# A GRU after attention on one core: input parts two steps at a time, accumulated in the gates' own PSUM banks

## The chip, the cores and the metric

The kernel runs on one core of a Trainium2 chip. The metric is the device time of one execution in microseconds (us). All arithmetic is in f32.

## The reference

Two layers with residual connections work on x of shape (16, 256, 512): batch B = 16, T = 256 steps, D = 512.

```python
x = x + _L0_cond_ref(x, cond[:, None, :], ...)   # normalisation, attention with 16 heads, o + o @ W_out
x = x + _L1_cond_ref(cond, x, W_ih, W_hh, b_ih, b_hh)

def cell(h, x):                                  # one step of the second layer, a GRU over T
    gi = x @ W_ih + b_ih                         # the input part
    gh = h @ W_hh + b_hh                         # the state part
    i_r, i_z, i_n = jnp.split(gi, 3, axis=-1)
    h_r, h_z, h_n = jnp.split(gh, 3, axis=-1)
    r = jax.nn.sigmoid(i_r + h_r)
    z = jax.nn.sigmoid(i_z + h_z)
    n = jnp.tanh(i_n + r * h_n)
    return (1.0 - z) * n + z * h
```

The first state is cond. The n gate's input part must stay apart from its state part, since only the state part is multiplied by r. Of r and z only the sum of both parts is needed. The 256 steps depend on each other through h.

## The kernel before, in words

The kernel has two stages. The attention stage takes the 16 batches one after the other; it ends at about 620 us in the profiled execution. The recurrent stage then runs the 256 steps. PE, DVE, ACT and POOL each follow the order in which the program was written (`manual_schedule`), so an instruction that waits holds all those behind it on its engine. SP issues the DMAs.

In the recurrent stage everything is held turned: the 512 features lie on 128 partitions in KC = 4 chunks, and 16 steps by 16 batches in the free dimension (`xT`, one tile for TI = 16 steps). Blocks of TG = 8 steps of x come in by DMA (`load_block`, six tiles `xin`), and DVE turns them into `xT` (`put_block`, L728). `output_step` (L713) makes the attention's output product for the next 16 steps in PSUM, and `put_output` (L746, DVE) adds it to `xT`. `input_step` (L713) makes the input parts `gi` for the next 16 steps: the weights `wih` are stationary, 128 x 32, and `xT` moves, 256 columns (16 steps x 16 batches); ACT adds the bias on the way out of PSUM (L757).

A step runs in this order.

1. PE: the state parts of r, n, z (`state_part`, L775). h is stationary, 128 x 16 for each k; the weights `whh` move, 128 columns, into four 32-column strips of the array, so 16 matmuls a gate. Each gate has one PSUM bank, of which 16 of every 32 rows are used.
2. DVE turns each gate back in 32 x 32 blocks (`turned`, L787), adds `gi` for r (L848), multiplies the state part of n by r (L851) and adds `gi` (L854), turns z and adds `gi` (L857).
3. ACT: sigmoid of r (L849), tanh of n (L855), sigmoid of z (L858). It also puts the n gate's hidden bias into its PSUM bank for the next step (`put_bhn`, L770).
4. PE, meanwhile: FILL = 4 steps of the products for the next 16 steps, by `output_step` or `input_step`.
5. DVE: three operations make the new h (L876 to L878). POOL adds h to x for the output (L880). Every eight steps DVE turns a block of output (L795) and SP stores it.

The group of the first 16 steps has no earlier steps to be made beside, so its `gi` is made before the first step; the last 16 steps have no next group to make.

An f32 matmul of the program is two instructions in the profile, and the four strips' matmuls go side by side.

Of the kernel before, what the change touches and what calls it, by code (L numbers as in the profile page):

```python
# [14 lines left out]
P = 128  # L15
# [4 lines left out]
def kernel(  # L20
# [35 lines left out]

    oT = const.tile([P, KC, T, B], F32, name="oT")
    wo = const.tile([P, KC, D], F32, name="wo")
    xin = ctx.enter_context(tc.tile_pool(name="xin", bufs=6))


    ada_a = const.tile([P, KC, B], F32, name="ada_a")
# [2 lines left out]
    gk_col = const.tile([P, 1], F32, name="gk_col")  # L65


    cond_sb = const.tile([KC * B, P], F32, name="cond_sb")
    for k in range(KC):
        nc.scalar.dma_start(cond_sb[k * B : (k + 1) * B, :], cond[:, k * P : (k + 1) * P])  # L70
    h0T = const.tile([P, KC, B], F32, name="h0T")

    work = ctx.enter_context(ExitStack())
    p1 = work.enter_context(tc.tile_pool(name="p1", bufs=1))
# [50 lines left out]
    def tile_ps(name, bank, shape=(P, D)):  # L125
        pool = ps if len(bank) == 1 else ps_lg
        return pool.tile(list(shape), F32, tag=bank, name=name)
# [313 lines left out]
    def slot2(b, w, prev, st):  # L441
        m = b + 1
        k = project(m, 1, 1, range(KC), "Y")
        maxima(w, range(HG))
        st.qk0 = norm_qk(m, 0, (st.q, st.k), st.rstd)
        st.v0 = project(m, 0, 2, (0,), "A")
        exps(w, range(HG))
        st.s1.add(0, st.sq)
        sq = st.s1.square(1, k)
        turn(prev)  # L450
        put_turned(prev, "vava")
        project(m, 0, 2, (1,), st.v0)
        st.s1.add(1, sq)
        if b + 3 < B:
            norm_first(b + 3, (1,))
        st.s1.rs.first()
        if b + 3 < B:
            batches[b + 3].rs.first()
        weigh(prev, "X")
        put_weighed(prev)  # L460
        if b == 0:

            for c in range(KC):
                d = wo[:, c, c * P : (c + 1) * P]
                nc.vector.tensor_tensor(d, d, ident, ALU.add)
        st.accs = (st.q1, k)
        st.rstd = st.s1.rs.second()
        normalize(w)
# [88 lines left out]
    with tc.manual_schedule(engines=ORDERED):  # L557
# [13 lines left out]
        for k in range(KC):  # L571
            for j in range(4):
# [4 lines left out]
                    start=(k == 0),  # L577
                    stop=(k == KC - 1),
                )
        cols = const.tile([P, 38], F32, name="cols")  # L580
        tp = tile_ps("tp_rows", "Y")
        nc.tensor.transpose(tp[:, :12], rows, ident[:12, :12])
        norm_first(0)
# [89 lines left out]
                    r = 32 * j + B * s  # L673
                    nc.sync.dma_start(xins[i][r : r + B], in_blocks(x, i, j, s))

    for i in range(6):
        load_block(i)


# [7 lines left out]
    gru = ctx.enter_context(tc.tile_pool(name="gru", bufs=2))  # L687


    bhn_rows = gru.tile([P, P], F32, name="bhn_rows", bufs=1)  # L690
    wide = gru.tile([P, KC, 32], F32, name="bhn_wide", bufs=1)
    nc.vector.tensor_copy(wide, bcols[:, 20:24].unsqueeze(2).to_broadcast([P, KC, 32]))
    nc.vector.transpose(bhn_rows, wide.rearrange("p q b -> p (q b)"))

    gates = []
    for name, bank in (("r", "A"), ("z", "X"), ("n", "Y")):
        gt = tile_ps(f"g{name}", bank, (P, P))
        nc.vector.memset(gt, 0.0)  # L700
        gates.append(gt)

    NI = T // TI
    NM = 3 * KC
    FILL = (KC + NM) * KC // TI
    gis = {}
    xTs = {}
    acc = {}

    def product(acc, w, m, k, rhs):  # L710

        for j in range(4):
            nc.tensor.matmul(  # L713
                acc[32 * j : 32 * j + 32, :],
                w[:, k, m * P + 32 * j : m * P + 32 * j + 32],
                rhs,
                start=(k == 0),
                stop=(k == KC - 1),
            )

    def put_block(i):

        grp, half = divmod(i, TI // TG)
        if half == 0:
            xTs[grp] = gru.tile([P, KC, TI, B], F32, tag="xT", name=f"xT_{grp}", bufs=3)
        nc.vector.transpose(  # L728
            xTs[grp][:, :, half * TG : (half + 1) * TG, :].rearrange("p q (s i) b -> p i q s b", s=2),
            xins[i],  # L730
        )
        load_block(i + 6)

    def output_step(grp, i):

# [9 lines left out]
        a = xTs[grp][:, m].rearrange("p t b -> p (t b)")  # L745
        nc.vector.tensor_tensor(a, o or acc["o"], a, ALU.add)  # L746

    def input_step(grp, i):

        m, k = divmod(i, KC)  # L750
        if i == 0:
            gis[grp] = gru.tile([P, NM, TI, B], F32, tag="gi", name=f"gi_{grp}")
        if k == 0:
            acc["i"] = tile_ps(f"gi_{grp}_{m}", ("Z", "lg2")[m % 2], (P, TI * B))
        product(acc["i"], wih, m, k, xTs[grp][:, k].rearrange("p t b -> p (t b)"))
        if k == KC - 1:
            nc.scalar.activation(  # L757
                gis[grp][:, m].rearrange("p t b -> p (t b)"), acc["i"], AF.Identity,
                bias=bcols[:, m : m + 1],
            )  # L760

    def open_hn():

        for j in range(4):
            nc.tensor.matmul(
                gates[2][32 * j : 32 * j + 32, :], ident[:, 0:32], ident, start=True, stop=True
            )

    def put_bhn():
        nc.scalar.copy(gates[2], bhn_rows)  # L770

    def state_part(g, hT):
        for k in range(KC):
            for j in range(4):
                nc.tensor.matmul(  # L775
                    gates[g][32 * j : 32 * j + B, :],
                    hT[:, k, :],
                    whh[:, k, g * D : (g + 1) * D].rearrange("p (q j c) -> p j q c", q=KC, c=32)[:, j],
                    start=(k == 0 and g != 2),
                    stop=(k == KC - 1),  # L780
                    skip_group_check=(g == 2),
                )

    def turned(g, t):

        tr = gru.tile([P, KC, 32], F32, tag=f"tr{g}", name=f"tr{g}_{t}")
        nc.vector.transpose(tr.rearrange("p q b -> p (q b)"), gates[g])  # L787
        return tr[:, :, 0:B]

    done = None  # L790

# [28 lines left out]
            queue.dma_start(dst[0, :, q], ol[0:B, q])  # L820

    with tc.manual_schedule(engines=ORDERED):
        for i in range(TI // TG):
            put_block(i)
        for i, o in enumerate(first):
            a = xTs[0][:, 2 * i : 2 * i + 2].rearrange("p q t b -> p q (t b)")
            nc.vector.tensor_tensor(a, o, a, ALU.add)  # L827
        for i in range(TI // TG, 2 * TI // TG):
            put_block(i)
        for i in range(NM * KC):  # L830
            input_step(0, i)
        open_hn()
        put_bhn()
        hT = h0T
        for t in range(T):
            tl = t % TG
            grp, ti = divmod(t, TI)
            gi = gis[grp]
            if tl == 0:
                y = gru.tile([P, KC, P], F32, tag="y", name=f"y_{t}", bufs=3)  # L840
            for g in (0, 2, 1):
                state_part(g, hT)

            def tile_of(name):
                return gru.tile([P, KC, B], F32, tag=name, name=f"{name}_{t}")

            r = tile_of("r")
            nc.vector.tensor_tensor(r, turned(0, t), gi[:, 0:KC, ti, :], ALU.add)  # L848
            nc.scalar.activation(r, r, AF.Sigmoid)  # L849
            n = tile_of("n")  # L850
            nc.vector.tensor_tensor(n, turned(2, t), r, ALU.mult)  # L851
            if t + 1 < T:
                put_bhn()
            nc.vector.tensor_tensor(n, n, gi[:, 2 * KC : 3 * KC, ti, :], ALU.add)  # L854
            nc.scalar.activation(n, n, AF.Tanh)  # L855
            z = tile_of("z")
            nc.vector.tensor_tensor(z, turned(1, t), gi[:, KC : 2 * KC, ti, :], ALU.add)  # L857
            nc.scalar.activation(z, z, AF.Sigmoid)  # L858


            ready = []
            if grp + 1 < NI:
                for i in range(FILL * ti, FILL * (ti + 1)):
                    if i < KC * KC:
                        output_step(grp + 1, i)
                        if i % KC == KC - 1:
                            ready.append((i // KC, acc["o"]))
                    else:
                        input_step(grp + 1, i - KC * KC)

            if t == T - 1:
                store_last(y, 0, TG - 1)


            h = gru.tile([P, KC, B], F32, tag="h", name=f"h_{t}", bufs=4)
            nc.vector.tensor_tensor(h, hT, n, ALU.subtract)  # L876
            nc.vector.tensor_tensor(h, h, z, ALU.mult)
            nc.vector.tensor_tensor(h, h, n, ALU.add)  # L878
            hT = h
            (nc.gpsimd if t + 1 < T else nc.vector).tensor_tensor(  # L880
                y[:, :, tl * B : (tl + 1) * B], xTs[grp][:, :, ti, :], h, ALU.add
            )
            for m, o in ready:
                put_output(grp + 1, m, o)
            block = t // TG + 2 * TI // TG
            if tl == TG - 2 and block < T // TG:
                put_block(block)
            if tl == 4 and done is not None:
                store(*done)
                done = None  # L890
            if tl == TG - 1:
                done = (t // TG, y)
        store_last(y, TG - 1, 1)
# [32 lines left out]
```

## Time and profile before

| | |
|---|---|
| time, median of 3 runs | 1775.45 us (1774.55 to 1776.77) |
| time of the profiled execution | 1775.52 us |
| span of its profile | 1773.7 us |
| PE busy | 1729.7 us, 98% |
| DVE busy | 1126.3 us, 64% |
| ACT busy | 816.9 us, 46% |
| POOL busy | 316.8 us, 18% |
| mean granted TensorE clock | 0.996 |
| first state part of step 0 | 644.22 us |
| first state part of step 1 | 648.57 us |
| first state part of the last step | 1763.54 us |

Span times count from the first instruction to the last; the profiled execution's own time is 1.8 us longer. A busy engine is not always the one that sets the end: PE's matmul ends are modelled, and whether PE or the loop through h sets a step must be read from the order of a step's instructions in time. Lines such as L775 are those of the kernel before; in the changed kernel the same functions stand at other lines.

### The profile page before, as it was taken

How to read it: one execution, taken by the hardware profiler on the slowest of the kernel's cores; microseconds unless marked ns; L12 is line 12 of the kernel's file. 1: busy time of each engine (PE TensorE's matmuls, PEld its weight loads, DVE VectorE, ACT ScalarE, POOL GpSimd, SP SyncE). 2: the span in 40 equal slices, each digit the busy share in tenths (PEclk: the TensorE clock that was granted, in tenths of full speed). 3: DMA queues.
4: the chain of work that ended last, by engine and by line, in shares of the span. 5: the costliest groups of instructions: out<-in, count | busy, mean ns of one | idle time of the engine just before them, and what ended most of it. 6: DMA issues, size and time to landing. Idle time of an engine off the chain costs nothing.

```text
span 1773.7 us, 91931 instructions
## 1 busy us (share of the span) xinstructions
PE 1729.7 (98%) x40755; PEld 1189.8 (67%) x40755; DVE 1126.3 (64%) x3703; ACT 816.9 (46%) x2760; POOL 316.8 (18%) x771
## 2 busy tenths in 40 slices
PE   7999999999999999999999999999999999999975
PEld 2444444444444578888888888888888888888865
DVE  4777777777776635656656656666556566665555
ACT  4777777777777623233233332333332332333322
POOL 0333344433344400000000000000000000000000
PEclk9999999999999899999999999999999999999999
DMA  8100000000000110100110011011101100000000
GB/s 286 38 14 14 14 26 14 14 14 23 5 3 2 73 27 16 22 16 16 22 22 16 17 23 20 16 20 22 17 16 21 22 10 10 16 10 10 10 15 14
DMA packets 146221, 43.72 MB, mean 25 GB/s; under 512 B 137899, under 2 KB 138031, under 8 KB 145823
## 3 DMA queue, kind: packets, MB, share of 16 engines
q1 hardware_dynamic: 145351, 36.73, 8.9%
q8 instruction: 320, 5.24, 1.2%
q10 hardware_dynamic: 472, 1.10, 0.2%
q14 instruction: 78, 0.64, 0.1%
HBM read 29.41 MB, written 8.39 MB: 21 GB/s over the span
## 4 chain that ended last, share of the span: by engine, by line
PE 94%; DVE 3%; ACT 1%; issue 1%; DMA 1%; DVEq 0%; ACTq 0%
PE qkv L214 19%; PE gi L713 18%; PE gr L775 13%; PE gn L775 13%; PE gz L775 11%; PE o L713 6%; PE tpa L188 4%; PE lg L279 4%; PE o L358 4%; PE tpqk L188 1%; DVE tr L787 1%; ACT attn L301 1%; PE tpx L188 1%; PE first L506 0%; DMA x<-in_x_dram 0%
## 5 line engine op out<-in xcount | busy, mean ns | idle before, releaser
L713 PE MATMUL gi<-xT,wih 128*32 128x256 f32 x6144 | 364.7, 379 | 0.0
L214 PE MATMUL qkv<-wq,xnT 128*32 128x512 f32 x3072 | 356.3, 598 | 0.6 <-DVE xnT L206 0.6
L312 POOL TENSOR_SCALAR attn<-attn,rden 128x256 f32<-128x256 f32 x510 | 234.1, 484 | 378.5 <-DVE rden L309 254.6
L775 PE MATMUL gr<-whh,h 128*16 128x128 f32 x8160 | 272.2, 274 | 24.1 <-DVE h L878 23.6
L880 POOL TENSOR_TENSOR y<-xT,h 128x64 f32<-128x64 f32 x255 | 82.0, 321 | 1068.0 <-DVE h L878 1033.1
L775 PEld LDWEIGHTS gr<-whh,h 128*16 128x16 f32 x8160 | 200.5, 96 | 107.1 <-DVE h L878 107.1
L775 PE MATMUL gz<-whh,h 128*16 128x128 f32 x8160 | 269.5, 273 | 0.0
L775 PE MATMUL gn<-whh,h 128*16 128x128 f32 x8160 | 269.5, 273 | 0.0
L301 ACT ACTIVATE attn<-lg,neg 128x256 f32<-128x256 f32 x512 | 234.9, 484 | 66.1 <-DVE neg L295 49.1
L713 PEld LDWEIGHTS gi<-xT,wih 128*32 128x32 f32 x6144 | 195.7, 110 | 101.3 <-DVE xT L827 0.7
L849 ACT ACTIVATE r<-r 128x64 f32<-128x64 f32 x256 | 65.7, 257 | 378.7 <-DVE r L848 378.7
L787 DVE STREAM_TRANSPOSE tr<-gr 128x128 f32<-128x128 f32 x256 | 81.1, 317 | 237.7 <-PE gr L775 237.7
L775 PEld LDWEIGHTS gn<-whh,h 128*16 128x16 f32 x8160 | 224.7, 97 | 0.0
L775 PEld LDWEIGHTS gz<-whh,h 128*16 128x16 f32 x8160 | 224.7, 97 | 0.0
L214 PEld LDWEIGHTS qkv<-wq,xnT 128*32 128x32 f32 x3072 | 87.4, 109 | 182.4 <-issue 157.3
L295 DVE TENSOR_REDUCE neg<-lg 128x2 f32<-128x512 f32 x256 | 159.1, 683 | 49.8 <-PE lg L279 49.8
L757 ACT ACTIVATE gi<-gi,cols 128x256 f32<-128x256 f32 x192 | 91.2, 475 | 164.1 <-PE gi L713 157.6
L787 DVE STREAM_TRANSPOSE tr<-gn 128x128 f32<-128x128 f32 x256 | 81.2, 317 | 76.0 <-PE gn L775 76.0
L341 DVE COPY attnT<-tpa 128x512 f32<-128x512 f32 x128 | 82.4, 682 | 59.2 <-ACT sq L225 34.6
L713 PE MATMUL o<-oT,wo 128*32 128x256 f32 x1920 | 114.6, 379 | 0.0
L855 ACT ACTIVATE n<-n 128x64 f32<-128x64 f32 x256 | 65.5, 256 | 98.5 <-DVE n L854 97.2
L301 ACT ACTIVATION_READ_ACCUMULATOR attn<-lg,neg 128x1 f32 x512 | 110.6, 216 | 0.0
(106 smaller groups left out, 1728.4 us busy)
## 6 DMA issues: line engine op xcount, KB each, us to landing
x<-in_x_dram SPq DMA_DIRECT2D x16, 512.0 KB, 4.0
xin<-in_x_dram SPq DMA_DIRECT2D x256, 32.0 KB, 2.0
out_dram<-osb SPq DMA_DIRECT2D x248, 32.0 KB, 1.8
wq<-in_L_cond_W_qkv_dram SPq DMA_DIRECT2D x12, 256.0 KB, 4.7
wih<-in_L_cond_W_ih_dram SPq DMA_DIRECT2D x4, 768.0 KB
whh<-in_L_cond_W_hh_dram SPq DMA_DIRECT2D x4, 768.0 KB
we<-in_L_cond_W_emb_dram SPq DMA_DIRECT2D x2, 512.0 KB, 4.8
we<-in_L_cond_W_emb_dram ACTq DMA_DIRECT2D x2, 512.0 KB
```

Of the source, the lines that this page charges most:

```text
L188: nc.tensor.transpose(dst[r], src[q], ident[q, q])
L214: nc.tensor.matmul(a[32 * j : 32 * j + 32, :], batches[b].xnT[:, k, n * P + 32 * j : n * P + 32 * j + 32], wq[:, k, s * D : (s + 1) * D], ...
L279: nc.tensor.matmul(w.lg[i][:, n, :], qT[r, g, n * P : (n + 1) * P], kT[r, g, :], start=True, stop=True,)
L295: nc.vector.tensor_reduce(w.neg[:, i, :], w.lg[i], AX.X, ALU.max, negate=True)
L301: nc.scalar.activation(a[:, n, :], w.lg[i][:, n, :], AF.Exp, bias=w.neg[:, i, n : n + 1], accum_out=w.den[:, i, n : n + 1],)
L312: engine.tensor_scalar(w.attn[i][:, n, :], w.attn[i][:, n, :], w.rden[:, i, n : n + 1], 1.0, ALU.mult, ALU.mult,)
L341: (nc.scalar.copy if engine is nc.scalar else nc.vector.tensor_copy)(dst, w.turned[i])
L713: nc.tensor.matmul(acc[32 * j : 32 * j + 32, :], w[:, k, m * P + 32 * j : m * P + 32 * j + 32], rhs, start=(k == 0), stop=(k == KC - 1),)
L757: nc.scalar.activation(gis[grp][:, m].rearrange("p t b -> p (t b)"), acc["i"], AF.Identity, bias=bcols[:, m : m + 1],)
L775: nc.tensor.matmul(gates[g][32 * j : 32 * j + B, :], hT[:, k, :], whh[:, k, g * D : (g + 1) * D].rearrange("p (q j c) -> p j q c", q=KC, c ...
L787: nc.vector.transpose(tr.rearrange("p q b -> p (q b)"), gates[g])
L880: (nc.gpsimd if t + 1 < T else nc.vector).tensor_tensor(y[:, :, tl * B : (tl + 1) * B], xTs[grp][:, :, ti, :], h, ALU.add)
```

## The change

The input parts are no longer made for 16 steps ahead and kept in SBUF. They are made for pairs of steps, one pair ahead, with x as the stationary operand (128 x 32: two steps of 16 batches) and the weights `wih` moving, 128 columns. They are accumulated in the PSUM banks in which the state parts follow. For r and z, input and state part sum up in the bank. The n gate's bank has two halves: the input part (with its bias) and the state part (with its bias).

- Each gate has two banks, for even and odd pairs. ACT seeds the banks of the next pair with the biases (`seed`, three copies every second step). `open_gate` does this by matmul for the first two pairs.
- In the first step of a pair the state part goes to rows 0 to 15 of each 32; in the second to rows 16 to 31, for which h is written into the second half of a tile whose first half is zero (`padded`), so that its stationary operand is 32 columns wide.
- DVE no longer adds `gi` to r and z; ACT reads the turned gate. In the first step of each pair DVE also turns the n gate's input half (`ni`), ahead of the turn of r, for both steps.
- Per step PE fills with one output step, two steps earlier than a step's share would be, and six input parts. Before the loop only the first pair's parts are made, and the rest of the first blocks' work moves into steps 0 and 1.
- `xin` has four tiles instead of six. The bias rows are made in the attention stage (`slot2` of batches 1 to 4, two small DVE operations each). The sigmoid table is loaded on ACT at the start of the stage.

```diff
+    gates = [
+        [tile_ps(f"g{name}_{i}", banks[i], (P, w, P)) for i in range(2)]
+        for name, banks, w in (("r", ("A", "lg2"), 1), ("z", ("X", "lg3"), 1), ("n", "ZY", 2))
+    ]
...
+    def seed(p):
+
+        nc.scalar.copy(gates[R_][p % 2][:, 0, :], b_rows[:, 0, :])
+        nc.scalar.copy(gates[N_][p % 2], b_rows[:, 2:4, :])
+        nc.scalar.copy(gates[Z_][p % 2][:, 0, :], b_rows[:, 1, :])
+
+    def gate_part(dst, rows, w, g, k, stationary):
         for j in range(4):
             nc.tensor.matmul(
+                dst[32 * j : 32 * j + rows, :],
+                stationary,
+                w[:, k, g * D : (g + 1) * D].rearrange("p (q j c) -> p j q c", q=KC, c=32)[:, j],
+                start=False,
+                stop=True,
+                skip_group_check=True,
             )
...
+    def input_part(p, g, k):
+
+        grp, ti = divmod(2 * p, TI)
+        x2 = xTs[grp][:, k, ti : ti + 2, :].rearrange("p t b -> p (t b)")
+        gate_part(gates[g][p % 2][:, 0, :], 32, wih, g, k, x2)
+
+    def state_part(t, g, hT):
+
+        dst = gates[g][t // 2 % 2]
         for k in range(KC):
+            gate_part(dst[:, dst.shape[1] - 1, :], hT.shape[2], whh, g, k, hT[:, k, :])
...
+            if s == 0 and p > 0 and more:
+                seed(p + 1)
+            if t > 0:
+                for g in (R_, N_, Z_):
+                    state_part(t, g, padded[p % 2] if s else hT)
...
+            gr, gz, gn = (gates[g][p % 2] for g in range(3))
+            if s == 0:
+                ni = turned("i", t, gn[:, 0, :])
             r = tile_of("r")
-            nc.vector.tensor_tensor(r, turned(0, t), gi[:, 0:KC, ti, :], ALU.add)
-            nc.scalar.activation(r, r, AF.Sigmoid)
+            nc.scalar.activation(r, turned("r", t, gr[:, 0, :])[:, :, s, :], AF.Sigmoid)
             n = tile_of("n")
-            nc.vector.tensor_tensor(n, turned(2, t), r, ALU.mult)
-            if t + 1 < T:
-                put_bhn()
-            nc.vector.tensor_tensor(n, n, gi[:, 2 * KC : 3 * KC, ti, :], ALU.add)
+            nc.vector.tensor_tensor(n, turned("h", t, gn[:, 1, :])[:, :, s, :], r, ALU.mult)
+            nc.vector.tensor_tensor(n, n, ni[:, :, s, :], ALU.add)
             nc.scalar.activation(n, n, AF.Tanh)
             z = tile_of("z")
-            nc.vector.tensor_tensor(z, turned(1, t), gi[:, KC : 2 * KC, ti, :], ALU.add)
-            nc.scalar.activation(z, z, AF.Sigmoid)
+            nc.scalar.activation(z, turned("z", t, gz[:, 0, :])[:, :, s, :], AF.Sigmoid)
...
+            for u in range(t + 2 if t else 0, t + 3):
+                if u // TI + 1 < NI:
+                    output_step(u // TI + 1, u % TI)
+                    if u % KC == KC - 1:
+                        ready.append((u // TI + 1, u % TI // KC, acc["o"]))
+            if more:
+                for g, k in parts[6 * s : 6 * s + 6]:
+                    input_part(p + 1, g, k)
...
-            h = gru.tile([P, KC, B], F32, tag="h", name=f"h_{t}", bufs=4)
+            if s == 0:
+                h = padded[p % 2][:, :, B:]
+            else:
+                h = gru.tile([P, KC, B], F32, tag="h", name=f"h_{t}", bufs=4)
```

## The prediction

> **What bounds the kernel now.** I read the page first, then one step of the recurrent stage in the timeline, then the two ends of that stage. The change touches nothing else of weight, so only these decide.
>
> The page's chain and its groups say PE, but not how narrowly:
>
> ```profile
> PE 94%; DVE 3%; ACT 1%; issue 1%; DMA 1%; DVEq 0%; ACTq 0%
> L775 PE MATMUL gr<-whh,h 128*16 128x128 f32 x8160 | 272.2, 274 | 24.1 <-DVE h L878 23.6
> ```
>
> The second line is the one to distrust: PE idles only 24.1 us for h over 255 steps, which looks like a PE bound. One step in the timeline (start, duration, engine, line) shows that it is not:
>
> ```profile
> 920.79 1.07 PE L775 MATMUL gr<-whh,h 128*16 128x128 f32 x32
> ...
> 921.92 0.32 DVE L787 STREAM_TRANSPOSE tr<-gr 128x128 f32<-128x128 f32 x1 [0.57 <-PE gr L775]
> 922.27 0.22 DVE L848 TENSOR_TENSOR r<-tr,gi 128x64 f32<-128x64 f32 x1
> ...
> 922.59 0.26 ACT L849 ACTIVATE r<-r 128x64 f32<-128x64 f32 x1 [1.10 <-DVE r L848]
> 922.80 0.32 DVE L787 STREAM_TRANSPOSE tr<-gn 128x128 f32<-128x128 f32 x1 [0.30 <-PE gn L775]
> ...
> 923.22 0.23 DVE L851 TENSOR_TENSOR n<-tr,r 128x64 f32<-128x64 f32 x1
> ...
> 923.48 0.22 DVE L854 TENSOR_TENSOR n<-n,gi 128x64 f32<-128x64 f32 x1
> 923.67 0.32 DVE L787 STREAM_TRANSPOSE tr<-gz 128x128 f32<-128x128 f32 x1
> 923.80 0.26 ACT L855 ACTIVATE n<-n 128x64 f32<-128x64 f32 x1 [0.38 <-DVE n L854]
> 924.02 0.23 DVE L857 TENSOR_TENSOR z<-tr,gi 128x64 f32<-128x64 f32 x1
> 924.16 0.22 DVE L876 TENSOR_TENSOR h<-h,n 128x64 f32<-128x64 f32 x1
> 924.34 0.26 ACT L858 ACTIVATE z<-z 128x64 f32<-128x64 f32 x1 [0.29 <-DVE z L857]
> 924.63 0.23 DVE L877 TENSOR_TENSOR h<-h,z 128x64 f32<-128x64 f32 x1 [0.25 <-ACT z L858]
> 924.89 0.22 DVE L878 TENSOR_TENSOR h<-h,n 128x64 f32<-128x64 f32 x1
> 925.17 0.68 PEld L775 LDWEIGHTS gr<-whh,h 128*16 128x16 f32 x28 [0.32 <-DVE h L878]
> ```
>
> A step is 925.17 - 920.79 = 4.38 us, and the next gr begins 0.06 after the last add of h: the chain ends last. The ends of the stage prove it, the first fence being its start, the second a step near its end:
>
> ```profile
> 623.26 20.93 PE L713 MATMUL gi<-xT,wih 128*32 128x256 f32 x384
> 644.00 0.40 PE L765 MATMUL gn<-ident 128*32 128x128 f32 x8
> 644.22 1.06 PE L775 MATMUL gr<-whh,h0T 128*16 128x128 f32 x32
> 646.84 1.91 PE L713 MATMUL o<-oT,wo 128*32 128x256 f32 x32
> 648.57 1.06 PE L775 MATMUL gr<-whh,h 128*16 128x128 f32 x32
> ```
>
> ```profile
> 1746.02 1.07 PE L775 MATMUL gr<-whh,h 128*16 128x128 f32 x32 [1.56 <-DVE h L878]
> ```
>
> In the last 16 steps PE has no filling work and waits 1.56 us each, yet they too last 4.38. So the chain is 4.38 and PE's own work fits in it almost exactly. PE's paces: each f32 matmul is two instructions, and four (one for each 32-column strip) go as a set. At 256 columns 96 sets take 644.00 - 623.26, or 0.216 us each. At 128 columns the 24 state sets take 646.84 - 644.22, or 0.109. A step's PE work is 24 x 0.1092 + 8 x 0.2158 = 4.35.
>
> **PE's work after.** The input parts turn from 256 columns (x moving) to 128 (weights moving), twice as many: per step 24 state sets, 12 input sets and 2 output sets, 36 x 0.1092 + 2 x 0.2158 = 4.36 us. Halving the columns costs 2 x 0.1092 - 0.2158 = 0.003 per pair of sets, about 0.01 a step. The Trainium skill speaks against it: "TensorEngine Tiling (Array Packing)", Instruction Overhead, puts about 60 cycles on each matmul; an estimate at the 2.4 GHz of "TensorE: Matmul & The Clock Gate" is 25 ns for each of six added sets a step, 0.15 us. The paces above leave no room for that, so I use them.
>
> The stationary operand becomes 32 columns wide for the input parts and for the state parts of odd steps (padded h); it is 16 now. The nearest row is L765, 32 wide at 128 columns: two sets from 644.00 to 644.22, the same 0.11. Its loads last 110 ns against 97 for 16 columns, which is just the pace of a set, so I take nothing and keep 3 ns a set as the upper bound. A gain is excluded, since columns already set the pace.
>
> **The chain in odd steps** (second of a pair). The additions at L848 and L857 go. Offsets from the start of gr: tr r 1.13 to 1.45 and straight to ACT, off the path, because the n gate is turned only at 2.01. Then n x r 2.43, n add 2.69, tanh 3.01 to 3.26, tr z 2.88 to 3.20. Sigmoid z starts at 3.29 instead of 3.55 (a DVE result reaches ACT in 0.10). Multiply 3.58, add 3.84 to 4.07, next gr 4.12. PE needs 4.36, so PE ends last: 4.36.
>
> **The chain in even steps** holds the cost. There a third transpose, ni, stands first on DVE. In the built order it waits for the last matmul of the n gate's *state* part, though it reads only the input half: both halves are one tile in one bank. The two transposes behind it carry no wait of their own, which fits only if the first one's wait covers the state part. So the turn of r, ready at 1.13, stands in the queue until 2.01, and ACT's sigmoid r waits for it. The "PSUM — Partial Sum Buffer" page, section Terms, gives a reason to keep such accesses apart: two engines on one bank and quadrant at once are an error there; no run here shows that.
>
> Working it out: DVE starts independent work about 0.08 before the former ends (z add 924.02, h subtract 924.16), so a transpose follows another after 0.24. ni 2.01, tr r 2.25 to 2.56, sigmoid r 2.66 to 2.91, tr n done 2.80. n x r starts 2.95 (ACT to DVE is 0.03), against 2.43 now. n add 3.21; tr z 3.35 to 3.67; tanh 3.53 to 3.78; sigmoid z 3.80 to 4.05 behind it. The subtract comes at 3.81 to 3.88 (0.03 or 0.10 after tanh), multiply 4.08 to 4.14, add 4.34 to 4.40, end 4.56 to 4.62, next gr 4.62 to 4.68. I take 4.67, since DVE's double wait costs 0.10 in the n row (923.12 to 923.22). Wide bounds: 4.54 if each handover is shortest and DVE overlaps more, 4.80 if transposes don't overlap at all (0.35 apart).
>
> **The sum**, against the profiled execution (1775.52 us, span 1773.7; the median of the runs is 1775.45, the same for this purpose).
> - Start of the stage: 20.7 us of input products go; in their place stand three gates with opening, state and input parts: 56 sets x 0.1092 = 6.1, from 623.2 to 629.3. Then step 0 fills with 8 opening sets, 6 output sets and 12 input sets, 3.48 us, and its chain (tr z at 629.6, h about 631) lies beside them. Step 1 starts at 632.8 instead of 648.57: -15.8.
> - Steps 1 to 237, fully filled: 119 odd x 4.363 + 118 even x 4.67 = 1070.3, against 237 x 4.38 = 1038.1: +32.2.
> - Steps 238 to 254: output steps have ended, PE needs 3.93 or less, the chain decides: 9 x 4.67 + 8 x 4.12 = 75.0 against 74.5: +0.5.
> - Last step, odd, shorter chain: -0.3.
>
> Together +16.6: 1775.5 + 16.6 = 1792.1, say 1792.
>
> **What I cost at nothing, and its cover.** Seeding copies on ACT, three every second step, at most 0.27 + 0.47 + 0.27 = 1.01 us by the 128x128 and 128x256 ACT rows: they run from the last sigmoid z (3.55) to 0.2 into the even step, whose sigmoid r comes at 2.66. Without that cover each would cost what it overhangs, up to 1.0 x 127 = 127 us. PE's wait for seeds comes after the state parts, long after. put_output (0.42) and the block transposes (0.70) run before DVE's first turn at 1.13 or 2.01. Input blocks are fetched 32 steps ahead instead of 48, 140 us against a landing of 2.0 us; SP only issues them earlier or later. At the start two more loads follow the first blocks, and block 4 is needed 25 us on. The four small broadcast-and-turn pairs in attention are 0.2 + 0.28 us each; PE leads there: 0, at most 2 us. The removed bias activations (91 us of ACT), the seeding of the n bias in each step and the memsets lay beside other work.
>
> **The rivals.**
> 1. *Forecast, the held transpose:* 1792, own range 1780 to 1804 (even steps at 4.57 to 4.76). For it: the order of waits, and durations of rows that stay. Chance 0.75.
> 2. *The hold does not bite, PE sets every step, faster:* if ni, or the turn of r, gets through before the n gate's state part, even steps fall to PE's 4.36. Then steps 1 to 237 give -4.0, the following 17 give -4.4, with -15.8 and -0.3: -24.5, 1751. It decides once even steps are below 4.54, since 16.6 / 127 = 0.13. Against it: the wait in the built order. For it: ni's data are ready a whole step earlier. Chance 0.09.
> 3. *Nothing measurable:* even steps come out at 4.51 to 4.57, the shortest handovers, and the saved start pays for them: 1772 to 1779. Chance 0.06.
> 4. *Wide loads set the pace besides:* 36 sets of an odd step at 112 ns instead of 109 are 0.10 x 119 = 12: 1804, and more if loads of four strips get in each other's way. For it: 110 ns of load against 109 of pace. Against it: the L765 sets. Chance 0.10.
>
> That the change does not do what it says is excluded for the sums (in the built order each pair's input parts stand in the pair before), and is case 1 for their reading.
>
> The range takes the lower end from case 1 and the upper one from case 4: 1780 to 1808. Faster by over 0.2% (3.5 us, about what a measurement of this kernel can tell from no change) is case 2, 0.09; within it case 3, 0.06; slower cases 1 and 4, 0.85.
>
> **What would show each step.** Steps alternating, about 4.67 and 4.36, seen in the starts of gr. In even steps three transposes at 2.0, 2.25 and 2.5 after gr, the first released by PE gn, and PE idle about 0.3 for h; in odd steps no idle. Gates' matmul sets still at 0.109. First step's gr gone and step 1 at about 633. The prediction is wrong if ni starts before 1 us into even steps (case 2), if odd steps exceed 4.40 with PE never idle (case 4), or if sigmoid r in even steps follows a seeding copy rather than its transpose.

## The result, and the profile after

The changed kernel takes 1911.71 us (median of 4 runs, 1911.55 to 1911.95) against 1775.22 of the kernel before (median of 4): a ratio of 1.0768, 95% interval 1.0749 to 1.0786. The forecast was 1792, with a range of 1780 to 1808. The direction was right, and the size is wrong by a factor of eight: 136.5 us longer instead of 16.6.

The first two views of the page already say where to look. These are PE's busy tenths in 40 slices of the span, first before and then after the change, and the chain that ended last after it:

```profile
PE   7999999999999999999999999999999999999975
```

```profile
PE   6888888888888999999999999999999999999997
...
PE 65%; ACT 15%; DVE 15%; issue 3%; DMA 1%; DVEq 0%; ACTq 0%
```

PE carries 65% of the chain instead of 94%, and in slices 2 to 13 it is busy for 80 to 89% of the time instead of 90% or more. That is the attention stage, of which the prediction costed only four small pairs of DVE operations, at 2 us at most. The same stretch of that stage, before and after (start and end, length, then busy us and instructions of each engine, granted TensorE clock, DMA share, GB/s):

```profile
45.00:600.00 555.00, 553.40 (x7450) 260.35 (x7446) 406.46 (x920) 427.02 (x1445) 224.97 (x491) 1.00 0.07 20
```

```profile
45.00:600.00 555.00, 483.42 (x6220) 215.12 (x6212) 343.37 (x785) 447.15 (x1271) 178.92 (x392) 0.97 0.05 14
```

The engines stand in the order PE, PEld, DVE, ACT, POOL. PE idles 72 us there instead of 2, and ACT was already busy for 427 of the 555 us before the change. The groups on ACT (line, operation, count, busy us, mean ns, idle before) and the start of ACT's timeline show why. Before the change the groups hold two loads of an activation table:

```profile
L559 ACT ACT_TABLE_LOAD x1 | 1.3, 1283 | 5.3 <-DMA cond_sb<-in_cond_dram 5.3
L849 ACT ACT_TABLE_LOAD x1 | 1.3, 1283 | 0.0
```

After it they hold 99, these among them:

```profile
L148 ACT ACT_TABLE_LOAD x48 | 61.6, 1283 | 0.8
L149 ACT ACT_TABLE_LOAD x48 | 61.6, 1283 | 0.8
L874 ACT ACT_TABLE_LOAD x1 | 1.3, 1283 | 9.2 <-DVE trr L799 9.2
```

```profile
12.16 0.19 ACT L171 ACTIVATION_READ_ACCUMULATOR xs<-x 128x1 f32 x1
12.37 1.28 ACT L835 ACT_TABLE_LOAD   x1
13.66 1.28 ACT L148 ACT_TABLE_LOAD   x1
14.95 0.29 ACT L148 ACTIVATE y_x<-ssx,eps 128x2 f32<-128x2 f32 x1
15.26 1.28 ACT L149 ACT_TABLE_LOAD   x1
16.56 0.20 ACT L149 ACTIVATE y_x<-y_x 128x2 f32<-128x2 f32 x1
```

L148 is the logarithm and L149 the exponential of the reciprocal square root (L142 and L143 before). Each now loads its table first, 96 loads of 1.283 us, 123 us of ACT. L835 is the line that loads the sigmoid table "at the start of the stage". It did not run there, but at 12.4 us, ahead of the first logarithm, and the load that it was to spare the recurrent stage still comes, at the first sigmoid (L874). Who waits for it, from the waits of the attention stage, before and then after (total us, times, longest):

```profile
DVE u_qk L147 <- ACT y_qk L143: 11.7, 29, 0.4
```

```profile
DVE u_qk L153 <- ACT y_qk L149: 81.2, 32, 2.9
PE qkv L220 <- ACT oT L375: 75.0, 28, 3.2
```

The recurrent stage nearly did what was forecast. An odd step, an even step and the beginning of the next odd one:

```profile
956.43 1.08 PE L775 MATMUL gr<-whh,padded 128*32 128x128 f32 x32 [0.15 <-DVE padded L907]
...
957.33 1.06 PE L775 MATMUL gn<-whh,padded 128*32 128x128 f32 x32
...
960.82 1.06 PE L775 MATMUL gr<-whh,h 128*16 128x128 f32 x32
...
961.69 1.06 PE L775 MATMUL gn<-whh,h 128*16 128x128 f32 x32
...
962.82 0.32 DVE L799 STREAM_TRANSPOSE tri<-gn 128x128 f32<-128x128 f32 x1 [2.26 <-PE gn L775]
963.06 0.27 DVE L799 STREAM_TRANSPOSE trr<-gr 128x128 f32<-128x128 f32 x1
963.25 0.28 DVE L799 STREAM_TRANSPOSE trh<-gn 128x128 f32<-128x128 f32 x1
...
963.42 0.26 ACT L874 ACTIVATE r<-trr 128x64 f32<-128x64 f32 x1 [2.77 <-DVE trr L799]
...
963.71 0.22 DVE L876 TENSOR_TENSOR n<-trh,r 128x64 f32<-128x64 f32 x1 [0.18 <-ACT r L874]
...
965.51 0.75 PE L775 MATMUL gr<-whh,padded 128*32 128x128 f32 x20 [0.15 <-DVE padded L907]
```

The odd step lasts 4.39 us and the even one 4.69. In the even one the three transposes (tri is the prediction's ni) stand at 2.00, 2.24 and 2.43 after gr, the first released by PE gn.

The split of the loss: the same group of four logits matmuls near the end of the attention stage begins at 720.15 us instead of 603.24 (before first, then after):

```profile
603.24 0.71 PE L279 MATMUL lg<-kT,qT 32*128 32x256 f32 x4
```

```profile
720.15 0.71 PE L285 MATMUL lg<-kT,qT 32*128 32x256 f32 x4
```

That is 116.9 later. The rest of the 136.2 us between the spans, 19.3, comes behind it, the recurrent stage for the most part.

### The profile page after: what moved, and what is told of

The parts are those of the page before. It is cut to its first block, busy times and chain, and to the rows that moved or that the text cites. A ratio compares the mean times of both kernels' runs of the same rounds, so it can differ in the third digit from the quotient of the medians.

```text
span 1909.9 us, 103872 instructions
## 1 busy us (share of the span) xinstructions
PE 1773.9 (93%) x46955; PEld 1347.9 (71%) x46955; DVE 1032.8 (54%) x3324; ACT 859.4 (45%) x2787; POOL 315.4 (17%) x773
## 4 chain that ended last, share of the span: by engine, by line
PE 65%; ACT 15%; DVE 15%; issue 3%; DMA 1%; DVEq 0%; ACTq 0%
PE gn L775 15%; PE qkv L220 15%; PE gr L775 13%; PE gz L775 12%; ACT attn L307 3%; PE o L719 3%; PE tpa L194 3%; ACT L149 2%; ACT L148 2%; DVE tri L799 2%; DVE neg L301 2%; PE lg L285 2%; ACT n L878 2%; ACT r L874 2%; ACT attnT L347 2%
## 5 line engine op out<-in xcount | busy, mean ns | idle before, releaser
L874 ACT ACTIVATE r<-trr 128x64 f32<-128x64 f32 x256 | 65.5, 256 | 645.8 <-DVE trr L799 642.7
L775 PE MATMUL gr<-whh,padded 128*32 128x128 f32 x4096 | 138.8, 276 | 25.2 <-DVE padded L907 22.7
L775 PE MATMUL gn<-wih,xT 128*32 128x128 f32 x4096 | 160.0, 273 | 0.0
L775 PE MATMUL gr<-wih,xT 128*32 128x128 f32 x4096 | 136.5, 273 | 0.0
L775 PE MATMUL gz<-wih,xT 128*32 128x128 f32 x4096 | 136.2, 273 | 0.0
L775 PE MATMUL gz<-whh,padded 128*32 128x128 f32 x4096 | 135.7, 273 | 0.0
L775 PE MATMUL gn<-whh,padded 128*32 128x128 f32 x4096 | 135.7, 273 | 0.0
L775 PEld LDWEIGHTS gn<-wih,xT 128*32 128x32 f32 x4096 | 120.7, 110 | 20.3
L775 PE MATMUL gr<-whh,h 128*16 128x128 f32 x4064 | 134.6, 273 | 0.3
L775 PE MATMUL gn<-whh,h 128*16 128x128 f32 x4064 | 134.5, 273 | 0.0
L775 PE MATMUL gz<-whh,h 128*16 128x128 f32 x4064 | 134.5, 273 | 0.0
```

Source lines behind the costliest of these rows:

```text
L775: nc.tensor.matmul(dst[32 * j : 32 * j + rows, :], stationary, w[:, k, g * D : (g + 1) * D].rearrange("p (q j c) -> p j q c", q=KC, c=32)[ ...
L874: nc.scalar.activation(r, turned("r", t, gr[:, 0, :])[:, :, s, :], AF.Sigmoid)
```

## The experiments

**The table line taken out of the changed kernel, and put alone into the kernel before.**

```diff
-        nc.scalar.preload_act_table_set("sigmoid_and_others")
```

> The changed kernel without its one line that loads the sigmoid table ahead of the recurrent stage. Theory T (table loads): that load stands at 12.4 us in the changed kernel's profile, ahead of the whole attention stage, and turns 0 loads there into 96 (123 us of ACT). Without it there are 2 loads in all, the attention slots fall back to 8.7 to 10.1 us (from up to 13.8), and the time falls by about 110 to 117 us to 1795 to 1800. The recurrent stage stays as in the changed kernel: steps of about 4.70 and 4.39 us. Rival D (the new DVE work for the bias rows in attention, or the smaller input pool, slows attention): attention stays slow and the time stays at about 1910. Rival M (both): something between, above 1810.

Measured: 1798.61 us (1797.84 to 1801.06), ratio to before 1.0124 (1.0109 to 1.0139). Two table loads are left:

```profile
L573 ACT ACT_TABLE_LOAD x1 | 1.3, 1283 | 5.3 <-DMA cond_sb<-in_cond_dram 5.3
L873 ACT ACT_TABLE_LOAD x1 | 1.3, 1283 | 9.2 <-DVE trr L799 9.2
```

The group of logits matmuls that was followed above begins at 603.6 us, as before the change (603.2), with the new DVE work for the bias rows and the smaller input pool still in. D and M fall.

```diff
     with tc.manual_schedule(engines=ORDERED):
+        nc.scalar.preload_act_table_set("sigmoid_and_others")
         for i in range(TI // TG):
             put_block(i)
```

> The kernel before with that one line alone added at the same place. Theory T: the attention stage gets 96 table loads and lasts about 117 us longer, the recurrent steps stay at 4.38 us, and the time is 1885 to 1895. Rival D: nothing happens to attention, since none of the other changes is in; 1775.

Measured: 1890.87 us (1889.56 to 1893.25), ratio 1.0643 (1.0627 to 1.0658). The groups of ACT:

```profile
L142 ACT ACT_TABLE_LOAD x48 | 61.6, 1283 | 0.8
L143 ACT ACT_TABLE_LOAD x48 | 61.6, 1283 | 0.8
...
L823 ACT ACT_TABLE_LOAD x1 | 1.3, 1283 | 0.0
```

That group of logits matmuls begins at 720.2. One line, in either kernel, is worth 113 us: 1890.87 - 1777.37 (the kernel before on that chip) = 113.5 in the one, and between spans 1909.9 - 1797.1 = 112.8 in the other. That is 9 in 10 of its 123 us of loads. The loads need not account for all of it directly: in the stretch of 45 to 600 us the granted clock was 0.97 with the early load in the changed kernel, 0.99 without it and 1.00 in the kernel before. How much of the 113 us comes by way of the clock was not separated.

**Which property of the line.** The same line with the set that holds logarithm and exponential.

```diff
-        nc.scalar.preload_act_table_set("sigmoid_and_others")
+        nc.scalar.preload_act_table_set("natural_log_exp_and_others")
```

> The changed kernel with the same early load at the same place, but of the table set that holds both the logarithm and the exponential, instead of the sigmoid's. Theory T1 (it matters which set is active when the first logarithm comes): no loads between logarithms and exponentials, three loads in all, attention slots as in the kernel before, and the time of the run without the line, 1795 to 1802. Rival T2 (a second early load, of whatever set, makes the kernel load at each use): 96 loads and about 1911.

Measured: 1799.26 us (1795.44 to 1800.98), ratio 1.0123 (1.0103 to 1.0143). L835 is still there, a load like any other, and L148 and L149 have none:

```profile
L573 ACT ACT_TABLE_LOAD x1 | 1.3, 1283 | 5.3 <-DMA cond_sb<-in_cond_dram 5.3
L835 ACT ACT_TABLE_LOAD x1 | 1.3, 1283 | 0.0
L874 ACT ACT_TABLE_LOAD x1 | 1.3, 1283 | 9.2 <-DVE trr L799 9.2
```

T1 holds, T2 falls. As long as the common set is active at the first logarithm, nothing is loaded between them. With the sigmoid's active there, a load stands ahead of all 48 logarithms and all 48 exponentials that follow them, so the set loaded for the one did not serve the other, and the common one did not come back. Which sets these were the profile does not name. Why the line moves ahead of the attention stage was not tried. What the runs show is that its place in the source did not hold it.

**The held transpose.** All without the table line. First, ni ahead of the state parts, so that it waits for the input part alone.

```diff
+            if s == 0:
+                ni = turned("i", t, gates[N_][p % 2][:, 0, :])
             if t > 0:
                 for g in (R_, N_, Z_):
                     state_part(t, g, padded[p % 2] if s else hT)
...
-            if s == 0:
-                ni = turned("i", t, gn[:, 0, :])
```

> The changed kernel without the table line, and with the turn of the n gate's input half (ni) issued ahead of the step's state parts, so that it waits only for the input part and stands on DVE right behind the former h. Theory H (the held transpose alone makes even steps long): even steps fall from 4.70 to PE's pace, 4.36 to 4.39, odd ones stay there; ni starts before 0.6 us into the step; the time is 1752 to 1758, faster than the kernel before by 1.0 to 1.3%, all of it from the start and the last 17 steps. Rival S (the extra transpose and the seeds themselves cost, wherever they stand): even steps stay above 4.5 and the time is 1775 or more.

Measured: 1763.36 us (1759.55 to 1769.33), ratio 0.993 (0.9903 to 0.9956). An even step and the start of the next:

```profile
863.96 0.31 DVE L799 STREAM_TRANSPOSE tri<-gn 128x128 f32<-128x128 f32 x1
863.97 1.06 PE L775 MATMUL gr<-whh,h 128*16 128x128 f32 x32
...
865.09 0.32 DVE L799 STREAM_TRANSPOSE trr<-gr 128x128 f32<-128x128 f32 x1 [0.83 <-PE gr L775]
...
868.33 1.06 PE L775 MATMUL gr<-whh,padded 128*32 128x128 f32 x32
```

The even step falls from 4.70 to 4.36 us and so does the odd one (median 4.362), and PE hardly waits. These are all of its waits from 640 to 1670 us (total us, times, longest; "issue" means that it waited for nothing that the profile shows):

```profile
PE gz L775 <- issue: 1.2, 4, 0.3
PE gr L775 <- DVE tri L799: 0.4, 1, 0.4
PE o L719 <- PE gz L775: 0.3, 1, 0.3
```

H holds for the steps, S falls. The time is some 5 us above the range that I expected; the last experiment looks at that.

Second, the order of the transposes alone: ni stays behind the state parts, but the turn of r goes first.

```diff
-            if s == 0:
-                ni = turned("i", t, gn[:, 0, :])
             r = tile_of("r")
             nc.scalar.activation(r, turned("r", t, gr[:, 0, :])[:, :, s, :], AF.Sigmoid)
+            if s == 0:
+                ni = turned("i", t, gn[:, 0, :])
```

> As the former, but ni is issued behind the turn of r and ahead of the turn of the n gate's state half: it still waits for the n gate's state part, and only the turn of r no longer stands behind it. Theory H in its finer form (the cost is the turn of r and its sigmoid standing behind the wait, not the wait): the product n x r starts at about 2.65 instead of 2.89, even steps last about 4.40, and the time is 1755 to 1764. Rival W (the wait for the state part costs by itself): even steps stay at about 4.70 and the time at 1795 to 1800.

Measured: 1766.17 us (1765.73 to 1769.42), ratio 0.9943 (0.9928 to 0.9958).

```profile
1059.47 1.06 PE L775 MATMUL gr<-whh,h 128*16 128x128 f32 x32
1060.59 0.32 DVE L799 STREAM_TRANSPOSE trr<-gr 128x128 f32<-128x128 f32 x1 [1.05 <-PE gr L775]
...
1061.47 0.32 DVE L799 STREAM_TRANSPOSE tri<-gn 128x128 f32<-128x128 f32 x1 [0.56 <-PE gn L775]
1061.71 0.28 DVE L799 STREAM_TRANSPOSE trh<-gn 128x128 f32<-128x128 f32 x1
...
1062.09 0.23 DVE L875 TENSOR_TENSOR n<-trh,r 128x64 f32<-128x64 f32 x1
...
1063.89 0.32 PE L775 MATMUL gr<-whh,padded 128*32 128x128 f32 x4
```

n x r starts at 2.62 (2.65 expected), and the even step lasts 4.42. ni starts 2.00 into the step here, exactly as in the changed kernel, yet 0.28 of the 0.34 us are gone. W falls: most of the cost was the turn of r behind the waiting instruction, not the wait.

**The best version once more.**

> The kernel with ni ahead of the state parts and without the table line once more, with more rounds, since its four times lay between 1759.6 and 1769.3. Theory F (where PE never waits for h, stalls at its own instruction fetches are no longer covered): steps at 4.362 us but for some fifty single ones that are 0.1 to 0.6 longer, at other steps than in the first profile of this kernel, in sum 10 to 18 us, each stall at the same distance from an instruction fetch; the time varies by several us from run to run, median 1760 to 1767. Rival B (stalls come from block loads and stores): they stand in the steps that issue them, tl 4 to 7 of each eight, and at the same steps as in the first profile.

Measured: 1762.22 us (1757.66 to 1762.24), ratio 0.9911 (0.9895 to 0.9927): this version is 0.9% faster than the kernel before. In its profiled run 41 of the steps 4 to 236 are longer than the median by over 0.01 us, 7.4 us in sum, fewer than I expected; in the first profile there were 102, 15.2 us in sum, without the one step in which PE waits for DVE. By the same count, for even and odd steps apart, the kernel before has 14, 2.4 us in sum, and the changed kernel without the table line 8, 1.2 us: where PE waits for h, few steps are longer. Of the steps with over 0.05 us extra, 66 in the first and 29 in the second, 12 are common. The 41 lie at all places of the eight-step pattern (3 to 8 steps at each), so B falls. Between the starts of PE's matmuls, halts of over 40 ns beyond the usual distance sum to 11 us in the first profile and 6 in the second; they end between 1.0 and 1.7 us ahead of the next transfer of queue 8, which carries instructions, most of them 1.1, in both profiles. The transfers of this queue (number, MB, share of 16 engines' time), the kernel before first and then this run:

```profile
q8 instruction: 320, 5.24, 1.2%
```

```profile
q8 instruction: 368, 6.03, 1.5%
```

On average they come every 4.39 us there in the recurrent stage and every 3.70 here. The ratio is that of PE's matmul rows in a step, 152 here against 128 there, which fits PE's own instruction stream. That halts and transfers share a rhythm is shown; that the halts are PE running out of instructions is argued from it, and was not tried by itself. Theory F stays unproven to that extent, and its sum came out lower than forecast.

## Why the prediction was wrong, point by point

**The step that failed** is in its first paragraph: "The change touches nothing else of weight, so only these decide." The change loads a table on ACT, and the prediction gave it no term, no cover and no place. It is 113 of the 120 us by which the forecast missed. The direction would have come out as forecast without it, since the kernel without the line still takes 1798.61 us, 7 us above the forecast; most of the measured loss has a cause that the prediction did not have. The loads are instructions of the program: ACT runs 99 of them against 2, and the one of L835 stands ahead of the first logarithm. I had read the built order for DVE and PE in the recurrent stage, where I expected the trouble, and not counted the operations of each engine over the whole program.

The Trainium skill bears on it. "ScalarE: Activation LUTs", section Table sets, says that tables are loaded as named sets and lists a set with both exponential and logarithm, so that a logarithm followed by an exponential needs one load. The run with the other table agrees (none between them); the changed kernel does not, with two loads for each such pair. Its section "What ACT_TABLE_LOAD costs" gives 1283 ns for a load, which is the mean here, and some 1380 ns more for a drain. The drain does not appear: in the timeline above a load follows its predecessor within 0.02 us and the activation follows as closely. By the page's 2.66 us, 96 switches would be an estimated 255 us of ACT; here they are 123, and the stage lost 117.

**The recurrent stage, by the sum's terms**, read from the kernel without the table line (span 1797.1 against 1773.7, +23.4; forecast +16.6; with the 112.8 of the line this makes the 136.2):
- Start: step 1 begins at 632.72 us instead of 648.57, -15.85; forecast -15.8.
- From there to the last step's start: 1154.4 us against 1115.0, +39.4; forecast +32.7. Even steps last 4.70 instead of 4.67, since h's multiply follows its subtract by 0.33 and I had used 0.26 to 0.27; odd ones 4.386 instead of 4.363.
- Last step: -0.25; forecast -0.3.

**Odd steps.** The 0.023 us come from PE's restart after it stood for h: from gr to gn there are 0.90 us (956.43 to 957.33) against 0.87 in the even step, ahead of which PE does not stand. With ni moved, padded steps too last 4.362, so the wide load does not set the pace; rival 4 falls in the form it had.

**Rival 2's price** was 1751 if nothing holds the turn of r. With the hold taken away the two runs had medians of 1763 and 1762, and their profiled executions 1762.25 and 1757.66: the mechanism was right, for steps fall to PE's own work. The term that it lacked are the longer steps, 15 us in the first profile (which reached step 1 some 4 us earlier) and 7 in the second. That they show because PE no longer waits for h is argued from the counts above. The seeds, the put_output operations and the shorter input pool were costed at nothing, and the median step of 4.362 us, PE's own work by the prediction's sum, agrees with it. So it does with the pace of 0.109 us a set with half the columns.

## What to carry to other kernels

Before costing the stage that a change is about, count each engine's operations over the whole built program, before and after: an instruction without data dependences need not stand where the source puts it (here at 12.4 us instead of beyond 620), and a table load changes what later activations need. On an engine that works in order, ask of every instruction that waits what stands behind it and was ready earlier; exchanging two transposes was worth 0.28 us in every second step. When loop and PE are equally long, shortening the loop gains little more than the work that the ends of the stage can absorb.

## What the runs showed of the hardware that was not expected

An activation table load of 1.28 us comes with no visible drain beside it, and 96 of them cost 0.92 of their own busy time although ACT was busy for only 77% of the stretch of 45 to 600 us before. PE with hardly a wait is not smooth: 41 and 102 of 233 steps were longer in two profiles of one program, and its times spread over 12 us, where the kernel before, waiting each step, spreads over 5.
